# Mirrored blocks of a symmetric product laid out by VectorE before their way through HBM, with new buffer limits and due times of the planner

## The chip, the cores and the metric

One of the eight cores of a Trainium2 chip runs the kernel. The metric is the device time of one launch in microseconds; the time before is the median of three runs, 2388.51 us (2387.62 to 2388.9).

## The reference

Sixteen graphs of 1024 nodes with 128 features go through four layers; each layer normalises x over the features, applies relu, computes something with the graph's 1024 x 1024 adjacency matrix and adds the result to x. All is float32. What matters here:

```python
# layer 0, three times (i = 0, 1, 2), relu after all but the last
h   = h @ W + b
nh  = h / max(norm(h), EPS)
cos = einsum('bij,bkj->bik', nh, nh)            # symmetric, 1024 x 1024
h   = einsum('bpq,bqc->bpc', edge_weight * cos, h)
# layer 1: y = relu(((1 + eps) x + adj^T x) @ W1 + b1) @ W2 + b2
# layer 2: softmax of tanh(s1_i + s2_j) where adj > 0, times h
# layer 3
e   = einsum('bil,bkl->bik', h @ A, h)
e   = e + swapaxes(e, 1, 2)                      # symmetric, 1024 x 1024
att = softmax(where(adj > 0, e, 0), axis=1) * adj
h_prime = relu(einsum('bij,bjk->bik', att, h))   # then three gates of x and h_prime
```

So four times in each graph a symmetric 1024 x 1024 product is formed: in layer 0 for i = 0, 1, 2 and in layer 3.

## The kernel before, in words

Work is tiled in 128 x 128 blocks: a graph has 8 row blocks (index j), and every row of blocks is handled in two halves of four blocks (s = 0 and 1, 512 columns, one PSUM bank). The stages of a graph are named in the plan: T (the transposed adjacency, `adjT`), 0 with 00, 01, 02 (layer 0 and its three products), 1, 2 and 3 (the other layers).

In a product stage 00, 01 or 02 the chain is this. `project` (L1200) multiplies the transposed activations `hT` with the weights, in two halves `psP` of four blocks; VectorE scales them into `h` (L1244; L1547 in stage 00); TensorE transposes each half (`flip`, L1169, into `ps_hTn`) and ScalarE copies it out as `hTn` (L1222). `Square.row` (L1360) multiplies block j of `hTn` with the columns from the diagonal on. VectorE weights each half with the norms and `adjT` into `ew` (L1589), and `accumulate` (L1422) adds it into `acc`, one bank for each half of the columns; in stage 02 `accumulate_nodes` (L1433) does it in blocks. When the eighth `ew` is in, ScalarE copies each half of `acc` out as the `hT` of the next stage (L1222), and `project` begins again. Layer 3 does the same with `e3` (L1854, by the masks) in place of `ew`.

The blocks below the diagonal are not multiplied again. They come in two ways. Those in the four diagonal quarters are copied to `above` by ScalarE (L1392) and transposed by TensorE (L1370). The 16 blocks of the lower left quarter go, for all products of graphs 1 to 13, through VectorE and HBM: for j = 0 to 3 and s = 1, `Square.keep` transposes the 32 x 32 squares of four blocks with one VectorE instruction (L1382); after each odd j, `Square.send` writes two rows of blocks to HBM (L1402, one DMA of 512 KB, called `by_hbm`), and reads them back so that each square lies in its place (L1413, four DMAs of 128 KB, 32 partitions each, into `got`). For j = 4 to 7 and s = 0, `ew` or `e3` reads `got` in place of a PSUM bank. The pieces written are 512 bytes long, the pieces read back 128 bytes, 32 elements.

The transposed adjacency of a later graph comes the same way: four DMAs of 128-byte pieces for each row block (L1509), then a VectorE transpose of the squares in place (L1517) and a ScalarE pass that sums the rows (L1520).

The order of all work is made when the program is built, by the class `Plan`. Every piece of work is an `Op` with an engine, a cost in microseconds, what it reads and writes, and a due time: `graph * PERIOD + TIMES[name][n]`. `Plan.order` goes forward in model time; of the engine whose next work can start first it takes, among the ops that can start within `WINDOW`, the one that is due first. A buffer comes from a pool (`POOLS`), and `KINDS` says how many of a kind may be in use in all and by graphs later than the oldest unfinished one. The result is one list; each engine gets its instructions in that order, and waits for what they read. `TIMES` has entries of their own for the first two and the last two graphs.

Of the kernel before, what the change touches and what calls it, by code (L numbers as in the profile page):

```python
# [12 lines left out]
ALU = mybir.AluOpType  # L13
AX = mybir.AxisListType

P = 128
# [205 lines left out]
def tile_adj_preln(  # L222
# [102 lines left out]
    for load_it in first:  # L325
# [13 lines left out]
        "adjT": ("adjT", 16, 16), "adjL": ("adjL", 5, 5), "x": ("x", 3, 3), "w4": ("big", 11, 5),  # L339
        "chunk": ("big", 13, 11), "above": ("above", 2, 2), "got": ("got", 1, 1), "ps": ("bank", 8, 7),  # L340
        "acc": ("bank", 8, 7), "small": ("small", 7, 18), "row": ("row", 5, 6), "hbm": ("hbm", 3, 3),
# [5 lines left out]
        "T DMA raw <0": [49.7, -29.05, 16.55, 2.15, 37.95, 6.2, 10.3, 13.25],  # L347
        "T PE raw <0": [7.8, -3.3, -0.1, -1.05, 0.65, 10.35, 23.15, 14.4, 9.05, 23.7, 22, 29.65, 26.65, 30.6,
            38.9, 41],
        "T ACT adjT <0": [2.9, 32.7, 7.85, 8.05, 13.45, 9.6, 13.2, 15.2, 18.4, 28.65, 29.8, 34.35, 33.9,  # L350
            38.45, 39.6, 39.65],
        "T DVE su <0": [54],
        "x DMA x <0": [49.15, -28],
        "0 DVE st <0": [5.7, 4.2],
        "0 DVE mv <0": [9.65],
        "0 POOL rstd <0": [2.6],
        "0 DVE nb <0": [9.1],
        "0 DVE hn <0": [9.1],
        "0 ACT hn <0": [30.5],
        "0 PE ps <0": [-0.85, -4.05],  # L360
        "0 ACT hT <0": [-21.45, 7.65],
        "00 PE psP <0": [6.6, -12.45],
        "00 DVE h <0": [14.75, 13.15],
        "00 PE ps <0": [21.35, 2.95],
        "00 ACT hTn <0": [11.15, 11.6],
        "00 ACT sq <0": [5.15, 12.1],
        "00 DVE ss <0": [2.95, 17.5, 18.2],
        "00 POOL rn <0": [30.3],
        "00 PE sq <0": [4.2, 22.45, 6.05, 6.9, 12, 7.4, 9.35, -26.35, 5.2, 26.95, 20.6, 21.8, 29.65, 25.9,
            26.55, 27.25, 31.3, 42.4, 46.3, 24.05, 51.65, 46.5],  # L370
        "00 ACT above <0": [12.45, 21.55, 15.8, 17.1, 16.7, 22.75, 22.65, 30.8, 38.15, 35.2],
        "00 DVE ew <0": [20.65, 22.5, 22.6, 36.95, 26.95, 33.7, 29.1, 35.05, 29.6, 44.15, 35.25, 41.45, 48.8,
            51.7, 45.3, 54.4],
        "00 PE acc0 <0": [0, 11.1, 10.4, 9.05, 15.65, 16.65, 19.7, 23.2, 28.65, 45.65, 34.25, 39.85, 31.35,
            54.3, 44.2, 64.05],
        "00 POOL params <0": [35.05, 40.7, 43.85, 51.55, 56.35, 57.25, 76.7],
        "00 DMA params <0": [52.85],
        "00 DVE params <0": [65.65, 68.1, 68.15, 77.5, 77.95],
        "00 PE params <0": [50.55, 59.35, 66.9],
        "00 ACT hT <0": [51.3, 54],  # L380
        "01 PE psP <0": [47.6, 63.65],
        "01 DVE h <0": [69.95, 78.75],
        "01 PE ps <0": [61.05, 52.95],
        "01 ACT hTn <0": [69.25, 72.45],
        "01 ACT sq <0": [69.7, 71.15],
        "01 DVE ss <0": [76.45, 78.15, 75.45],
        "01 POOL rn <0": [84.25],
        "01 PE sq <0": [68.25, 64.9, 66.25, 69.95, 68.2, 60.6, 70.8, 71.45, 81.95, 78.25, 78.75, 81.15,
            80.55, 85.85, 84.35, 87.05, 85.5, 86.8, 87.75, 84.5, 87.75, 79.1],
        "01 ACT above <0": [72.2, 74.55, 76.2, 75.5, 83.2, 81.35, 84.35, 84.75, 92.9, 94.75],  # L390
        "01 DVE ew <0": [78.15, 92.4, 81.55, 86.8, 87.85, 85.5, 93, 91.7, 93.05, 101.05, 89.5, 98.7, 96.5,
            111.15, 94.25, 91.55],
        "01 PE acc0 <0": [72.7, 84, 78.85, 78.6, 79.65, 78.25, 84.45, 78.05, 85.7, 85.9, 84.65, 87.6, 87.45,
            91.5, 89.15, 92.05],
        "01 ACT hT <0": [97, 99.95],
        "02 PE psP <0": [92.4, 92.15],
        "02 DVE h <0": [111.65, 105.7],
        "02 PE ps <0": [94.65, 94.55],
        "02 ACT hTn <0": [109.1, 104.6],
        "02 ACT sq <0": [106.2, 98.2],  # L400
        "02 DVE ss <0": [108.35, 109.3, 110.85],
        "02 POOL rn <0": [131.5],
        "02 PE sq <0": [103.1, 100.15, 107.65, 110, 101.65, 105.05, 100.95, 91.9, 107.7, 108.8, 108.7, 114,
            114.45, 111, 117.45, 118.85, 121.8, 110.4, 111.4, 123.9, 120.8, 128.25],
        "02 ACT above <0": [109.85, 113, 103.2, 116.3, 113.65, 115.55, 120.5, 124.45, 131.85, 139.8],
        "02 DVE ew <0": [113.25, 106.15, 118, 112.45, 125.7, 120.05, 121.65, 124.9, 130.25, 128.35, 126.65,
            132.8, 124.95, 126.9, 123, 141.6],
        "02 PE acc0 <0": [90.15, 114.45, 106.85, 103.9, 110.45, 112.95, 116.3, 111.45, 125.35, 117.1, 121.95,
            130.1, 112.45, 124.05, 123.15, 120.6],
        "02 DVE x <0": [136.55, 141.55],  # L410
        "T DMA adjT <1": [-129, -138.55, -158.15, -107.7, -154.45, -138.3, -107.8, -104.7],
        "T DVE adjT <1": [-118.3, -111.9, -110.5, -104.85, -101.8, -89, -85.8, -85.05],
        "T ACT adjT <1": [-117.75, -118.25, -112.75, -111.85, -103.3, -98.6, -96, -94.9],
        "1 DVE st <0": [135.95, 138.05],
        "1 DVE mv <0": [141.5],
        "1 POOL rstd <0": [134.7],
        "1 DVE nb <0": [144.5],
        "1 DVE hn <0": [140.8],
        "1 ACT hn <0": [134.3, 134.75],
        "1 DVE x <0": [146.55, 166.45, 168],  # L420
        "1 DMA adjL <0": [49.7, 59.55, 62.4, 63.35, 48, 159, 152, 151.35],
        "1 DVE adjL <0": [80.85, 77.2, 82.45, 79, 78.25, 151.75, 156.5, 161.35],
        "1 PE acc1 <0": [134.5, 135.3, 136.2, 137, 138.5, 133.15, 142.35, 139.75, 142.8, 141.1, 147.5,
            146.05, 148.15, 145.4, 151.95, 150.35],
        "1 ACT g <0": [157.9, 152.5],
        "1 PE py <0": [148.1, 149.8, 154.65, 147.75],
        "1 ACT y1 <0": [150.4, 163, 157.05, 152.1],
        "1 PE py2 <0": [152.35, 154.2],
        "2 DVE st <0": [171.4, 171.55],
        "2 DVE mv <0": [176.05],  # L430
        "2 POOL rstd <0": [176.55],
        "2 DVE nb <0": [173.9],
        "2 DVE hn <0": [173.85],
        "2 ACT hn <0": [184, 172.8],
        "2 PE ps <0": [162, 177.1],
        "2 ACT hnT <0": [180.45, 171.9],
        "2 DVE alone <0": [56.3],
        "2 DVE x <0": [183.6, 216.45, 216.65],
        "2 PE psP <0": [180.2, 166.35, 167.75],
        "2 ACT h <0": [176.5, 180.2, 180.6],  # L440
        "2 DVE hrow <0": [176.1],
        "2 PE pf <0": [171.3],
        "2 ACT hfl <0": [183.15],
        "2 PE pt <0": [174.35],
        "2 ACT sr <0": [180.15],
        "2 DMA sd <0": [283.8],
        "2 DMA s1 <0": [230.2],
        "2 DVE h <0": [175.5],
        "2 ACT e2 <0": [186.9, 189.9, 184.6, 189.95, 190.8, 191.25, 189.25, 193.65, 194, 192.5, 194.7, 197.1,
            198.05, 200.15, 199.1, 197.05],  # L450
        "2 DVE e2 <0": [195.1, 187.55, 193.65, 194.5, 199.55, 199.6, 196.4, 198.2, 201.75, 200.6, 203.8,
            206.9, 206.25, 208.1, 207.45, 208.75],
        "2 PE acc2 <0": [186.85, 186.2, 184.15, 189.1, 194.4, 197.45, 194.9, 188.8, 187.75, 198.65, 189.3,
            188.2, 194.8, 201.05, 196.95, 200.75, 197.1, 199.85, 195.55, 197.6, 198.5, 195, 197.75, 199],
        "2 DVE rden <0": [210.05, 211, 214.85, 213.35],
        "3 DVE st <0": [214.65, 213.1],
        "3 DVE mv <0": [246.2],
        "3 POOL rstd <0": [230.15],
        "3 DVE nb <0": [191.15],
        "3 DVE hn <0": [197.2],  # L460
        "3 ACT hn <0": [220.35, 225.45],
        "3 PE ps <0": [220.35, 209.3, 217.3, 213.95],
        "3 ACT hnT <0": [217.95, 221.55],
        "3 PE pg <0": [214.85, 222.65],
        "3 ACT gT <0": [221.05, 225.75],
        "3 PE psP <0": [228.55, 206.05, 224.15],
        "3 DVE h <0": [228.15, 223.85, 227.05],
        "3 ACT h3T <0": [219.7, 220],
        "3 ACT mask <0": [8.25, 18.4, 14.05, 26, 16.05, 23.05, 27.85, 30.25, 28.2, 40.5, 248.85, 250, 222.55,
            229.15, 237.05, 239.9],  # L470
# [679 lines left out]
    def by_block(t, w=D, n=NB):  # L1150
        return t[:, 0 : n * w].rearrange("p (c d) -> p c d", d=w)
# [976 lines left out]
```

## Time and profile before, and how to read it

| | before |
|---|---|
| median of 3 runs | 2388.51 us |
| the profiled execution | 2389.48 us, span 2387.7 us |
| TensorE matmul busy | 2349.2 us, 98% of the span |
| VectorE busy | 2029.0 us, 85% |
| ScalarE busy | 1435.5 us, 60% |
| the 52 mirrored products through HBM: writes / reads | 104 DMAs of 512 KB / 416 of 128 KB |
| packets under 512 B / all | 1108441 / 1316743 |
| a steady graph, 617.3 to 1917.1 us, nine of them | 144.4 us |

The span runs from the first to the last instruction. A busy engine's records can overlap, so that what TensorE loses is better read from the starts: a record of a 512-column matmul normally starts 0.429 us after the one before (each float32 matmul has two records), one of 128 columns 0.111, a transpose of a block 0.109. What a start comes later than that is called a stall below. The first TensorE record starts 7.3 us after the span's start, the last ends 10.5 us before its end, and the stalls of over 0.02 us in between sum to 44.6 us.

### The profile page before, as it was taken

The page shows a single profiled execution, that of the slowest core. Times are in us where ns is not written, and L with a number is a line of the kernel's source. Part 1 is how long each engine was busy: PE and PEld are TensorE (multiplying, and loading weights), DVE is VectorE, ACT ScalarE, POOL GpSimd, SP SyncE. Part 2 cuts the span into 40 slices and gives each one's busy share as a digit, 9 for nine tenths or more (in the row PEclk, how much of TensorE's full clock was granted, in tenths as well). Part 3 has the DMA queues.
Part 4 walks back from the last instruction along what each step waited for, and adds up shares of the span by engine and source line. Part 5 has one row for each costly group of instructions (what it writes and reads, how often), then busy time and mean ns, then how long its engine had stood idle before and what let it go on. Part 6 is the DMA issues. An engine that isn't in the chain of part 4 may idle for free.

```text
span 2387.7 us, 35098 instructions
## 1 busy us (share of the span) xinstructions
PE 2349.2 (98%) x11577; PEld 1548.5 (65%) x11577; DVE 2029.0 (85%) x5570; ACT 1435.5 (60%) x2561; POOL 246.8 (10%) x168
## 2 busy tenths in 40 slices
PE   8999999999999999999999999999999999999997
PEld 5568566675766657666575666757576575765764
DVE  6658798898988989899898988989899888987676
ACT  7325765756566465755756657465765656655475
POOL 3001010100101101010100101001011010110012
PEclk9999999999999999999999999999999999999999
DMA  9342949879596886959779497796968869165000
GB/s 197 85 107 63 172 91 180 153 128 178 115 177 141 139 171 130 171 123 166 157 129 181 108 181 146 137 164 130 171 139 149 164 129 169 45 107 124 1 27 18
DMA packets 1316743, 314.31 MB, mean 132 GB/s; under 512 B 1108441, under 2 KB 1298017, under 8 KB 1316561
## 3 DMA queue, kind: packets, MB, share of 16 engines
q1 hardware_dynamic: 1296400, 301.35, 67.6%
q10 hardware_dynamic: 19264, 9.70, 1.4%
q8 instruction: 92, 1.51, 0.3%
q0 software_dynamic: 896, 1.01, 0.2%
q14 instruction: 91, 0.74, 0.1%
HBM read 227.50 MB, written 84.47 MB: 131 GB/s over the span
## 4 chain that ended last, share of the span: by engine, by line
PE 85%; DMA 5%; SPq 4%; ACT 3%; DVE 3%; issue 1%; DVEq 0%; ACTq 0%
PE acc L1422 33%; PE sq L1360 18%; PE acc L1433 17%; PE psP L1200 6%; PE sq L1370 4%; DMA by_hbm<-above 2%; PE py L1210 2%; DMA got<-by_hbm 2%; PE py L1651 2%; SPq L1413 1%; SPq L1509 1%; PE ps_hTn L1169 1%; PE pg L1210 1%; DVE ew L1589 1%; DMA adjT<-in_adj_dram 1%
## 5 line engine op out<-in xcount | busy, mean ns | idle before, releaser
L1422 PE MATMUL acc<-ew,h 128*128 128x512 f32 x1024 | 486.4, 597 | 8.0 <-DVE ew L1589 8.0
L1589 DVE SCALAR_TENSOR_TENSOR ew<-sq,rn,adjT 128x512 f32<-128x512 f32 x612 | 436.4, 740 | 59.4 <-PE sq L1370 24.4
L1360 PE MATMUL sq<-hTn 128*128 128x512 f32 (+3 forms) x1152 | 439.4, 488 | 0.8 <-ACT hTn L1222 0.4
L1392 ACT COPY above<-sq 128x384 f32<-128x384 f32 (+3 forms) x432 | 167.6, 393 | 365.1 <-PE sq L1370 263.1
L1360 PEld LDWEIGHTS sq<-hTn 128*128 128x128 f32 x1152 | 196.3, 191 | 148.0 <-issue 99.8
L1422 PEld LDWEIGHTS acc<-ew,h 128*128 128x128 f32 x1024 | 180.2, 191 | 169.9 <-issue 132.4
L1433 PEld LDWEIGHTS acc<-h,ew 128*128 128x128 f32 x2048 | 245.4, 192 | 35.9 <-issue 21.7
L1433 PE MATMUL acc<-h,ew 128*128 128x128 f32 x2048 | 253.3, 275 | 3.2 <-DVE ew L1589 3.2
L1433 PEld LDWEIGHTS acc<-h,e 128*128 128x128 f32 x2048 | 235.0, 192 | 17.2 <-issue 12.8
L1422 PE MATMUL acc<-e,hs 128*128 128x512 f32 x512 | 241.1, 594 | 1.3 <-ACT hs L1904 0.8
L1433 PE MATMUL acc<-h,e 128*128 128x129 f32 x2048 | 236.6, 275 | 1.1 <-DVE e L1763 1.1
L1422 PE MATMUL acc<-adjL,hn 128*128 128x512 f32 x512 | 232.9, 592 | 0.0
L1162 POOL TENSOR_TENSOR rstd<-ve,mhalf 128x8 f32<-128x8 f32 x64 | 105.0, 1641 | 1166.5 <-DVE ve L1281 1166.5
L1370 PEld LDWEIGHTS sq<-ident,above 128*128 128x128 f32 x960 | 124.4, 141 | 100.2 <-issue 76.5
L1854 DVE CUSTOM_DVE_ANT_0 e<-mask,sq 128x512 f32<-128x512 int8 x204 | 137.4, 680 | 60.6 <-ACT above L1392 53.2
L1520 ACT ACTIVATE adjT<-adjT 128x1024 f32<-128x1024 f32 x120 | 126.6, 1055 | 97.8 <-DVE adjT L1517 90.4
L1895 DVE TENSOR_TENSOR e<-e,adjT 128x512 f32<-128x512 f32 x248 | 166.1, 680 | 18.2 <-ACT e L1886 18.1
L1382 DVE STREAM_TRANSPOSE above<-sq 128x512 f32<-128x512 f32 x208 | 145.7, 706 | 35.5 <-PE sq L1360 35.5
L1370 PE MATMUL sq<-ident,above 128*128 128x128 f32 x960 | 172.5, 273 | 1.5 <-ACT above L1392 1.5
L1763 DVE SCALAR_TENSOR_TENSOR e<-adjT,e 128x512 f32<-128x512 f32 x256 | 162.3, 689 | 5.5 <-ACT e L1759 5.3
L1422 PEld LDWEIGHTS acc<-adjL,hn 128*128 128x128 f32 x512 | 93.6, 190 | 102.3 <-issue 90.9
L1517 DVE STREAM_TRANSPOSE adjT<-adjT 128x1024 f32<-128x1024 f32 x120 | 148.6, 1239 | 8.8 <-DMA adjT<-in_adj_dram 8.4
(164 smaller groups left out, 3587.2 us busy)
## 6 DMA issues: line engine op xcount, KB each, us to landing
adjL<-in_adj_dram SPq DMA_DIRECT2D x128, 512.0 KB
adjT<-in_adj_dram SPq DMA_DIRECT2D x480, 128.0 KB
by_hbm<-above SPq DMA_DIRECT2D x104, 512.0 KB
got<-by_hbm SPq DMA_DIRECT2D x416, 128.0 KB
s<-sd SPq DMA_DIRECT2D x15, 512.0 KB
out_dram<-z ACTq DMA_DIRECT2D x15, 512.0 KB
d_hT<-hn SPq DMA_DIRECT2D x14, 512.0 KB
hT<-d_hT SPq DMA_DIRECT2D x56, 128.0 KB
```

The costliest lines, as they stand in the source:

```text
L1200: nc.tensor.matmul(dst.t[:, (c - lo) * n : (c - lo + 1) * n], cols(srcT.t, c), w, start=True, stop=True)
L1360: lambda: nc.tensor.matmul(dst.t[:, (first - lo) * P :], cols(leftT.t, j), span(rightT.t, first, hi), start=True, stop=True),
L1370: nc.tensor.transpose(cols(dst.t, r), cols(above.t, p), ident)
L1382: lambda: nc.vector.transpose(span(above.t, p, p + 4), read.t),
L1392: lambda: nc.scalar.copy(span(above.t, p, p + hi - first), read.t[:, (first - lo) * P :]),
L1422: lambda s=s, lo=lo, hi=hi: nc.tensor.matmul(acc[s].t, cols(h.t, at, w), span(ew.t, lo, hi), start=(j == 0), stop=(j == NB - 1)),
L1433: nc.tensor.matmul(a.t[:, (c - lo) * n : (c - lo + 1) * n], cols(ew.t, c), h.t[:, at * w : at * w + n], start=(j == 0 and c == lo), stop=( ...
L1517: dve(V(N), [t], [t], lambda t=t: nc.vector.transpose(t.t, t.t), True)
L1589: lambda view=view, ew=ew, rn=rn, j=j, lo=lo, hi=hi: nc.vector.scalar_tensor_tensor(by_block(span(ew.t, lo, hi), D, 4), view(), rn.t[:, j ...
L1763: lambda e=e, j=j, lo=lo, hi=hi: nc.vector.scalar_tensor_tensor(span(e.t, lo, hi), span(aT[j].t, lo, hi), 0.0, span(e.t, lo, hi), op0=ALU. ...
L1854: lambda e=e, view=view, mask=mask, peak=peak, s=s, lo=lo, hi=hi: nc.vector.tensor_tensor_reduce(by_block(span(e.t, lo, hi), D, 4), by_blo ...
L1895: lambda e=e, j=j, lo=lo, hi=hi: nc.vector.tensor_mul(span(e.t, lo, hi), span(e.t, lo, hi), span(aT[j].t, lo, hi)),
```

## The change

Three parts.

1. VectorE's transpose of the squares (L1382, new L1385) reads and writes in another order: the four squares of a 32-row group that belong to one destination row group lie side by side in `above`, so that one piece of HBM holds runs for all four blocks. The write to HBM is as before in size and pieces (128 x 8 x 128). The read back has four DMAs as before, with pieces of 128 elements, 512 bytes, in place of 32 elements: the listing of the built program shows `got<-by_hbm 32x8x128 x4` for `32x32x32 x4`.
2. `got` then holds runs of 32 columns, which `ew` and `e3` read as 16 runs of 32 elements; a helper `like` gives the output and the other operand the same shape. No instruction is added for it. The planner's cost of the read falls from 3.6 to 1.8 for two rows.
3. All due times in `TIMES` and several limits in `KINDS` are new, so that the planner makes another order of the same work. In the listing TensorE has the same instructions as before, in another order; VectorE, ScalarE and GpSimd too, and the DMAs of the SP queue. In the steady graphs the order repeats from graph to graph, in both kernels.

```diff
-        "adjT": ("adjT", 16, 16), "adjL": ("adjL", 5, 5), "x": ("x", 3, 3), "w4": ("big", 11, 5),
-        "chunk": ("big", 13, 11), "above": ("above", 2, 2), "got": ("got", 1, 1), "ps": ("bank", 8, 7),
-        "acc": ("bank", 8, 7), "small": ("small", 7, 18), "row": ("row", 5, 6), "hbm": ("hbm", 3, 3),
+        "adjT": ("adjT", 16, 16), "adjL": ("adjL", 5, 5), "x": ("x", 3, 3), "w4": ("big", 9, 5),
+        "chunk": ("big", 10, 12), "above": ("above", 2, 1), "got": ("got", 1, 1), "ps": ("bank", 7, 8),
+        "acc": ("bank", 7, 8), "small": ("small", 7, 16), "row": ("row", 3, 3), "hbm": ("hbm", 3, 3),
...
-        "T DMA raw <0": [49.7, -29.05, 16.55, 2.15, 37.95, 6.2, 10.3, 13.25],
+        "T DMA raw <0": [51.6, -92.65, -42.9, 3.5, 39.85, 7.55, 4, 14.6],
...
+    def like(v, t):
+
+        return t.rearrange("p (x i) -> p x i", i=v.shape[2])
...
-                return self.got, lambda: self.got.t.rearrange("p (r c d) -> p c r d", r=QUARTER, d=P)[:, q]
+                return self.got, lambda: self.got.t.rearrange("p (x q i) -> p q x i", q=QUARTER, i=SQ)[:, q]
...
-                    lambda: nc.vector.transpose(span(above.t, p, p + 4), read.t),
+                    lambda: nc.vector.transpose(
+                        self.apart(j // 2).rearrange("p (h r q i) -> p r h q i", r=2, q=QUARTER, i=SQ)[:, j % 2],
+                        read.t.rearrange("p (q h i) -> p h q i", h=P // SQ, i=SQ),
+                    ),
...
+        def apart(self, pair):
+
+            return span(self.above.t, 6 + 8 * pair, 14 + 8 * pair)
...
-                src = by_hbm.t.rearrange("(x j) (g i) -> g j x i", j=SQ, i=SQ)
-                for g in range(P // SQ):
-                    dst = span(got.t, lo * 4, hi * 4)[g * SQ : (g + 1) * SQ]
-                    with nc.allow_non_contiguous_dma(reason="squares"):
-                        nc.sync.dma_start(dst.rearrange("p (x i) -> p x i", i=SQ), src[g])
-
-            op("DMA", 1.8 * (hi - lo), [by_hbm], [blk(got, lo * 4, hi * 4)], squares_to_places, lat=2.4)
+                src = by_hbm.t.rearrange("(h y j) f -> h j y f", h=P // SQ, j=SQ)
+                dst = by_block(span(got.t, lo * 4, hi * 4))
+                for h in range(P // SQ):
+                    nc.sync.dma_start(dst[h * SQ : (h + 1) * SQ], src[h])
+
+            op("DMA", 1.8, [by_hbm], [blk(got, lo * 4, hi * 4)], squares_to_places, lat=2.4)
...
-                            by_block(span(ew.t, lo, hi), D, 4), view(), rn.t[:, j : j + 1],
-                            by_block(span(aT[j].t, lo, hi), D, 4), op0=ALU.mult, op1=ALU.mult,
+                            like(view(), span(ew.t, lo, hi)), view(), rn.t[:, j : j + 1],
+                            like(view(), span(aT[j].t, lo, hi)), op0=ALU.mult, op1=ALU.mult,
```

TensorE's order in the steady graph 7, from the listing of the two built programs, where stage 01 begins (`acc0_7_0_1` is the second half of stage 00's sum, `psP_7_1_1` the second half of stage 01's projection, `ps_hTn_7_1_1` its transposes; names with 6 belong to layer 2 of the graph before):

```
before                                        after
acc0_7_0_1 <- ew_7_0_7   (the last one)        acc0_7_0_1 <- ew_7_0_6
ps_hnT_6_2_1 x4                                pt_6
psP_6_2_0 x3                                   ps_hTn_7_1_0 x4
psP_7_1_1 x4                                   acc0_7_0_1 <- ew_7_0_7   (the last one)
ps_hTn_7_1_0 x4                                psP_7_1_1 x4
psP_6_2_3 x3                                   ps_hTn_7_1_1 x4
psP_6_2_6 x2                                   sq_7_1_0_0
ps_hTn_7_1_1 x4                                sq_7_1_0_1
```

## The prediction

> **What bounds the kernel now.** I read the page first: the share of each engine and the chain that ended last.
>
> ```profile
> span 2387.7 us, 35098 instructions
> PE 2349.2 (98%) x11577; PEld 1548.5 (65%) x11577; DVE 2029.0 (85%) x5570; ACT 1435.5 (60%) x2561; POOL 246.8 (10%) x168
> PE 85%; DMA 5%; SPq 4%; ACT 3%; DVE 3%; issue 1%; DVEq 0%; ACTq 0%
> ```
>
> TensorE is busy for 98% and carries 85% of the chain. A busy record can hide a stall, so I went to the starts of the records: a 512-column record normally starts 0.429 us after the last, a 128-column one 0.111, a transpose 0.109. Summing what comes later than that gives 44.6 us of stalls, with 7.3 us before the first record and 10.5 after the last; the other 2325 us are streaming, which the change leaves alone, since TensorE's instructions are the same. So a gain can at most be some of 44.6 us, while a worse order has no such limit. Next, the busy time by stretches, one row for each steady graph:
>
> ```profile
> core 0: us, PE busy (x) PEld busy (x) DVE busy (x) ACT busy (x) POOL busy (x), PEclk, DMA share, GB/s
> 906.61:1050.37 143.76, 143.51 (x705) 94.42 (x705) 128.80 (x353) 89.66 (x158) 13.36 (x8) 1.00 0.81 150
> 1050.37:1195.95 145.58, 144.07 (x705) 94.32 (x705) 128.85 (x353) 88.95 (x158) 13.36 (x8) 1.00 0.85 149
> ```
>
> A graph takes 144.4 us on average; VectorE works 128.8 of it, so it has 15 us of room, and the 16 DMA engines are 81 to 85% busy. The stalls of these nine graphs are 0.7 to 2.5 us each. What makes them is in the timeline. A trip to ScalarE and back that is partly covered, 0.44 us of TensorE work lying between (graph 5, stage 02; the same in every steady graph):
>
> ```profile
> 783.73 2.74 PE L1422 MATMUL acc<-ew,h 128*128 128x512 f32 x6
> 786.31 0.60 PE L1169 MATMUL ps_hTn<-ident,h 128*128 128x128 f32 x4
> 787.16 2.94 PE L1200 MATMUL psP<-w,hT 128*128 128x128 f32 x24 [0.25 <-ACT hT L1222]
> ```
>
> The four transposes take 0.44 us; the projection starts 0.85 us after them, 0.41 more than normal. The same trip with nothing between, at the end of graph 14:
>
> ```profile
> 2334.76 4.45 PE L1422 MATMUL acc<-e,hs 128*128 128x512 f32 x10
> 2339.25 1.08 ACT L1222 ACTIVATE hpT<-acc 128x512 f32<-128x512 f32 x2 [7.61 <-PE acc L1422]
> 2339.89 2.05 PE L1200 MATMUL psN<-eye,hpT 128*128 128x131 f32 x16 [0.69 <-ACT hpT L1222]
> ```
>
> Here the stall is 0.85 us. And a trip to VectorE with four blocks' instructions, in graph 2, stage 01:
>
> ```profile
> 309.85 2.04 PE L1200 MATMUL psP<-w,hT 128*128 128x128 f32 x16
> 311.03 2.16 DVE L1244 SCALAR_TENSOR_TENSOR h<-psP,rn,b 128x128 f32<-128x128 f32 x8 [0.30 <-PE psP L1200]
> 311.73 1.85 PE L1169 MATMUL ps_hTn<-ident,h 128*128 128x128 f32 x8
> ```
>
> Eight transposes are normally 0.87 us of starts and end at 1.03; they take 1.85, because each waits for its block of `h`. Last, the mirrored blocks, late in graph 1:
>
> ```profile
> 58.20 7.13 SPq L1413 DMA_DIRECT2D got<-by_hbm  x8
> 69.48 2.74 DVE L1589 SCALAR_TENSOR_TENSOR ew<-got,rn,adjT 128x512 f32<-128x512 f32 x4 [8.23 <-DMA got<-by_hbm]
> 70.28 2.07 PE L1422 MATMUL acc<-ew,h 128*128 128x512 f32 x2 [4.25 <-DVE ew L1589]
> ```
>
> Eight reads keep the SP queue for 7.13 us, VectorE waits 8.23 us for them, and TensorE stalls 4.47 us. After that five records of 512 columns start 0.85 us apart.
>
> **What the Trainium skill says.** "DMA: Bandwidth & Descriptors", Specifications: 512 bytes is the smallest transfer at line rate. The packet records agree in kind: a 128-byte packet took 15.6 ns on average, a 512-byte one 28.5, so four times the bytes for 1.8 times the time. "Perfetto Trace Analysis", DMA Instruction (HWDGE): the issue's recorded span ends when the descriptors are made, not at the landing; here VectorE starts 4 us after the last of the eight issues. "TensorE: Matmul & The Clock Gate", Part 1 (The HAM clock gate): after an idle window of some 3.4 us the clock is halved until TensorE has been busy again; the five records at twice their time after 4.47 us agree. "SBUF — State Buffer", Door 1 (The DMA port swizzle): full bandwidth needs further accesses within a 16-byte line; runs of 32 elements (128 bytes) fill whole lines. No row of this trace reads or writes in runs of 32.
>
> **The change part by part.**
>
> *Transfers.* The 416 reads drop from 1024 packets to 256 each. For one pair of rows: 4096 x 15.6 / 16 = 4.0 us of the DMA engines becomes 1024 x 28.5 / 16 = 1.8; the four issues, 3.12 us at the median, become perhaps 4 x 0.39 = 1.6 (0.39 is the median issue of the 512-byte writes). The two overlap, so the way gets 1.6 to 2.2 us shorter. In a steady graph the first user in stage 00 has 12.3 us of TensorE work as lead and stalls for 0 to 0.8, so the way is 12.3 to 13.1 long; it becomes about 10.9. The new order gives it 11.2. That covers it, and I let all stalls at `got` in steady graphs go: 6.8 us in nine graphs, 0.76 each. At the head, eight issues fall from 7.1 to about 3.1 us; the lead falls from 13.0 to 11.8; the stall goes from 4.5 to 1.7, and with it the slow clock (5 x 0.42 = 2.1): a gain of 4.9. In graph 2, stage 01, the lead falls from 18.1 to 8.2 us; against 10.9 this costs some 2.5.
>
> *VectorE.* 16 transposes and 16 reads of `got` in a graph keep their counts. I take their rows (0.706, 0.748, 0.680 us); a gain is excluded, as engine, type and number of elements are the same, and above I keep twice the row.
>
> *Order.* Hidden or not is a matter of lead: the TensorE work that its own order puts between what a trip starts from and what waits for it. From the listing, a steady graph after the change has, with the prices above (first record and following ones):
> - stage 01, second half of `psP` directly behind the last `acc`: lead 0, 0.85 + 0.11 = 0.96;
> - stage 01, second half's transposes directly behind that: at lead 0.44 the case of graph 2 cost 0.15 + 0.45 = 0.60, so at lead 0 1.04;
> - stage 02, `psP` behind `acc` again: 0.96;
> - stage 02, transposes with lead 0.44: 0.60;
> - stage 00, a transposed block with lead 0.64: 0.14, as at the same lead in graph 1.
>
> Sum 3.70 us. Before there is one such place, 0.53. Work lies ready in neither case: in the new order nothing else stands between on TensorE's queue, and all behind waits. On VectorE's queue the second `h` of stage 01 now stands behind sums, statistics and aggregates of the next graph (0.68 + 0.10 + 4 x 2 x 0.21 + 0.64 + 0.17 = 3.3 us since the last `ew`, against 1.06 + 0.85 + 0.89 = 2.8 for TensorE's side), so it is 0.4 to 0.5 late; in stage 02 0.2. I add 0.5, bounds 0 and 0.7. Net for a steady graph: 3.70 + 0.5 - 0.53 - 0.76 = 2.9. Graphs 5 to 13: 9 x 2.9 = 26.2.
>
> *The other graphs*, by the same list: graph 2 3.7 + 2.5 against 4.1 (+2.1), graph 3 2.2 against 1.3 (+0.9), graph 4 2.8 against 0.7 (+2.1); graphs 0 and 1 +1.5 and the head's -4.9; graph 14 -0.3; graph 15 +1.7 (short leads around `ps_hTn`). Together +3.1. The last 10.5 us, and SP's moved loads (its issues shrink by 8 x 1.6 us a graph), I cost at nothing: the tail's instructions keep their order, and the loads have leads of tens of us.
>
> Sum: 26.2 + 3.1 = 29.3, on the profiled execution's 2389.5: 2418.8. That execution is 1.0 above the median, so 2417.8; I take 2418. Bounds: VectorE's lateness -4.5 to +2, head and graph 2 +-5, graph 15 +-4, so 2404 to 2436.
>
> **The rivals.**
> - *Faster: shorter transfers outweigh the bare trips.* Place: the users of `got`, and the small gaps of some 0.9 us a graph that VectorE, waiting 22.7 us for `got` in all, may be causing. Price: 11.8 us of stalls, 2.1 of slow clock, and up to 14 of small gaps, 28 together. It decides if the bare trips cost less than that, that is under some 2 us a graph; at half my price (18 in all) the time is 2378. For it speaks that the DMA engines are over 80% busy; against it that the trips are measured with the same instructions in the same trace, and that the small gaps stand at record boundaries.
> - *The reads do not get shorter* (landing, not packets, sets them). Then the lead of 11.2 is 1.1 short, and the 0.76 stays: 9 x 1.9 = 17, graph 2 another 2, the head 6: 2443. Against it: eight issues alone took 7 us.
> - *Runs of 32 make VectorE slow.* It decides from (147.3 - 128.8) / 32 = 0.58 us for each of the 32 instructions; at twice their rows VectorE has 151 us a graph, 13 x 7 us more: 2480. Against it: runs of 128 from `got` took 0.748 where runs from PSUM took 0.740.
> - *Nothing to be seen*: losses and gains cancel, 2388.
>
> **How the numbers follow.** Bare trips 0.81 (2418, own range 2404 to 2436), reads not shorter 0.08, faster 0.05, VectorE bound 0.04, cancelled 0.02. Leaving out all but the first keeps 0.81, so its range is the range. Within 0.2% (4.8 us, about what a measurement of this kernel can tell) I put 0.03.
>
> **What would show it.** Steady graphs of about 147.3 us; in each, `psP` twice with an idle time of some 0.7 us ended by ScalarE's `hT`, and `ps_hTn` ended by VectorE's `h` right behind; waits for `got` near zero; the four read issues at 1.6 us or less; `ew<-got` and the transposes at their old means. Steady graphs at 144.4 or below would prove the trips wrong, `got` waits of 1 us a graph the transfers, VectorE means above 0.9 us its pattern.

## The result, and the profile after

The changed kernel takes 2543.82 us (median of six runs, 2541.32 to 2547.84), the kernel before, beside it, 2388.7; the ratio is 1.065 [1.0635, 1.0662], so it is 155 us slower where 29 were forecast. The profiled execution took 2543.01 us. The new lines are 3 to 9 below the old ones. The page again first, its span, engines and chain:

```profile
span 2541.1 us, 35091 instructions
PE 2405.7 (95%) x11577; PEld 1565.6 (62%) x11577; DVE 2041.0 (80%) x5570; ACT 1438.4 (57%) x2561; POOL 251.0 (10%) x168
PE 71%; DVE 10%; DMA 7%; ACT 6%; SPq 3%; issue 2%; DVEq 0%; POOL 0%; ACTq 0%
```

No engine has much more to do, and TensorE's share of the chain fell from 85 to 71%: the time is in waits. By the starts of TensorE's records it is all there: the first starts at 7.25 us, the last ends at 2530.5, and the stalls of over 0.02 us sum to 198.2 (44.6 before), which leaves 2325.0 us of streaming, for 2325.3 before. By the graph whose work waits:

| TensorE's stalls, us | before | after | difference | forecast |
|---|---|---|---|---|
| graphs 0 to 4 | 21.7 | 96.1 | +74.4 | +1.7 |
| graphs 5 to 13 | 12.8 | 79.5 | +66.7 | +26.2 |
| graphs 14 and 15 | 10.0 | 22.6 | +12.6 | +1.4 |

Busy time by stretches, a steady graph and then the longest one of the start, from the first matmul of one graph's stage 00 to that of the next; the row after that is the same stretch of the start in the kernel of experiment 1, which has the new layout in the old order (by the counts of TensorE's records, 955 and 1005, the two stretches of the start do not hold quite the same work):

```profile
1617.34:1769.09 151.75, 147.10 (x705) 95.44 (x703) 128.57 (x349) 89.47 (x157) 13.41 (x8) 0.99 0.70 143
154.80:361.58 206.78, 190.78 (x955) 129.38 (x954) 150.25 (x425) 119.08 (x204) 15.98 (x9) 0.96 0.47 109
```

```profile
150.39:351.09 200.70, 198.92 (x1005) 132.58 (x1004) 163.13 (x469) 123.10 (x213) 16.94 (x10) 1.00 0.50 116
```

The steady graph was forecast at 147.3; graphs 5 to 13 take 152.1 on average. VectorE works 128.6 us in the one shown, as before, and the DMA engines are busy for 70%. Where it waits, the timeline of TensorE and then that of ScalarE show for graph 11, between stages 01 and 02:

```profile
1779.70 1.45 PE L1431 MATMUL acc<-ew,h 128*128 128x512 f32 x3
1783.55 1.16 PE L1203 MATMUL psP<-w,hT 128*128 128x128 f32 x8 [2.40 <-ACT hT L1225]
1784.54 1.71 PE L1172 MATMUL ps_hTn<-ident,h 128*128 128x128 f32 x8
```

```profile
1780.18 0.63 ACT L1575 ACTIVATE sq<-h 128x512 f32<-128x512 f32 x1 [2.47 <-DVE h L1247]
1780.85 1.65 ACT L1308 ACTIVATE hn<-x,nb,rstd 128x128 f32<-128x128 f32 x4
1782.40 0.61 ACT L1329 ACTIVATE hn<-hn 128x512 f32<-128x512 f32 x1
1782.92 0.57 ACT L1225 ACTIVATE hT<-acc 128x512 f32<-128x512 f32 x1
```

The copy `hT` that TensorE waits for is ready to go soon after the last `acc`, but five instructions `hn` of the graph before stand ahead of it. The wait at `got` has not gone either. The issues of its reads, its users on VectorE (shortest, median and longest one in ns), and what VectorE sat idle for before them (us, times), before and then after:

```profile
L1413 SPq DMA_DIRECT2D got<-by_hbm x416: 302/650/3469, 58.2 to 2135.1; - x139
  DMA got<-by_hbm: 22.7, 18
```

```profile
L1422 SPq DMA_DIRECT2D got<-by_hbm x416: 302/448/1927, 59.4 to 2274.8; - x139
L1598 DVE SCALAR_TENSOR_TENSOR ew<-got,rn,adjT x156: 710/747/767, 70.2 to 2115.8; 128x512 f32<-128x512 f32 x156
  DMA got<-by_hbm: 37.3, 19
```

The median issue of a read falls to 0.448 us (0.650 before), and the four of a pair to 1.80 (3.11); the aggregates, `ew` from `got`, take 0.747 us as before (0.748); but VectorE waits 37.3 us for `got`, where it was 22.7.

### The profile page after: what moved, and what is told of

It reads as the page before. It is cut to its first block, busy times and chain, and to the rows that moved or that the text cites. A ratio compares the mean times of both kernels' runs of the same rounds, so it can differ in the third digit from the quotient of the medians.

```text
span 2541.1 us, 35091 instructions
## 1 busy us (share of the span) xinstructions
PE 2405.7 (95%) x11577; PEld 1565.6 (62%) x11577; DVE 2041.0 (80%) x5570; ACT 1438.4 (57%) x2561; POOL 251.0 (10%) x168
## 4 chain that ended last, share of the span: by engine, by line
PE 71%; DVE 10%; DMA 7%; ACT 6%; SPq 3%; issue 2%; DVEq 0%; POOL 0%; ACTq 0%
PE acc L1431 27%; PE sq L1363 16%; PE acc L1442 14%; PE psP L1203 5%; PE sq L1373 3%; DVE ew L1598 3%; DMA by_hbm<-above 2%; SPq L1518 2%; DMA got<-by_hbm 2%; ACT e L1764 2%; PE py L1213 1%; PE ps_hTn L1172 1%; DVE x L1247 1%; ACT hn L1308 1%; DVE h L1247 1%
## 5 line engine op out<-in xcount | busy, mean ns | idle before, releaser
L1431 PE MATMUL acc<-ew,h 128*128 128x512 f32 x1024 | 499.9, 606 | 33.9 <-DVE ew L1598 33.4
L1363 PE MATMUL sq<-hTn 128*128 128x512 f32 (+3 forms) x1152 | 447.0, 493 | 0.2 <-ACT hTn L1225 0.2
L1442 PEld LDWEIGHTS acc<-h,e 128*128 128x128 f32 x2048 | 243.4, 195 | 42.0 <-DVE e L1772 20.1
L1442 PE MATMUL acc<-h,e 128*128 128x129 f32 x2048 | 248.0, 279 | 18.4 <-DVE e L1772 18.3
L1385 DVE STREAM_TRANSPOSE above<-sq 128x512 f32<-128x512 f32 x208 | 146.5, 707 | 54.3 <-PE sq L1363 54.0
```

Of the source, the lines that this page charges most:

```text
L1363: lambda: nc.tensor.matmul(dst.t[:, (first - lo) * P :], cols(leftT.t, j), span(rightT.t, first, hi), start=True, stop=True),
L1385: lambda: nc.vector.transpose(self.apart(j // 2).rearrange("p (h r q i) -> p r h q i", r=2, q=QUARTER, i=SQ)[:, j % 2], read.t.rearrange(" ...
L1431: lambda s=s, lo=lo, hi=hi: nc.tensor.matmul(acc[s].t, cols(h.t, at, w), span(ew.t, lo, hi), start=(j == 0), stop=(j == NB - 1)),
L1442: nc.tensor.matmul(a.t[:, (c - lo) * n : (c - lo + 1) * n], cols(ew.t, c), h.t[:, at * w : at * w + n], start=(j == 0 and c == lo), stop=( ...
```

## The experiments

Theory 1: the order loses the time, and the layout gains a little. Theory 2: the layout loses it. Then, within theory 1: why is the order poor, the due times (1b) or the price that the planner takes for a read (1a)? The limits play no part: with the old `KINDS` the changed kernel gets the same order on every engine.

**1. Layout alone**: the old `TIMES`, `KINDS` and planner's prices under the new transposes, DMAs and views; against the changed kernel:

```diff
-            op("DMA", 1.8, [by_hbm], [blk(got, lo * 4, hi * 4)], squares_to_places, lat=2.4)
+            op("DMA", 1.8 * (hi - lo), [by_hbm], [blk(got, lo * 4, hi * 4)], squares_to_places, lat=2.4)
...
-        "T DMA raw <0": [51.6, -92.65, -42.9, 3.5, 39.85, 7.55, 4, 14.6],
+        "T DMA raw <0": [49.7, -29.05, 16.55, 2.15, 37.95, 6.2, 10.3, 13.25],
...
```

> The new layout (transposes, writes, reads of 512-byte pieces, columns in runs of 32) with the old due times, limits and planner's costs: the listing of this kernel has the order of the kernel before on every engine. Theory 1 (the new order loses the time, the layout gains a little): the waits at got of the steady graphs and of the head go, 2374 to 2387 us. Theory 2 (the layout itself loses it: the reads land later, or runs of 32 hold VectorE up): 2450 to 2545. If the reads are shorter but their landing is as late as before: 2386 to 2391.

2377.67 us (2376.41 to 2377.88), ratio 0.995 [0.9939, 0.9964]. Theory 2 is out: the layout alone is 11 us, 0.5%, faster. Waits for `got` on VectorE are down to 8.2 us in all, 7.0 of them in the head; a steady graph takes 143.70 us (1214.26 to 1357.96), 0.7 less than before.

**2. Order alone**: the changed kernel's order with the old transposes, DMAs and views; against the kernel before:

```diff
-            op("DMA", 1.8 * (hi - lo), [by_hbm], [blk(got, lo * 4, hi * 4)], squares_to_places, lat=2.4)
+            op("DMA", 1.8, [by_hbm], [blk(got, lo * 4, hi * 4)], squares_to_places, lat=2.4)
...
-        "T DMA raw <0": [49.7, -29.05, 16.55, 2.15, 37.95, 6.2, 10.3, 13.25],
+        "T DMA raw <0": [51.6, -92.65, -42.9, 3.5, 39.85, 7.55, 4, 14.6],
...
```

> The old layout (128-byte pieces read, planner's prices as in the changed kernel) in the order of the changed kernel on every engine. Theory 1 (order): at least the changed kernel's time, and 1 to 2 us more in each of graphs 1 to 13, since the way through HBM is some 2 us longer and its lead of 11.2 us was already short: 2545 to 2580. Theory 2 (layout): near the kernel before, 2390 to 2440.

2622.94 us (2614.01 to 2636.8), ratio 1.098 [1.0951, 1.1017]: theory 1, and with more than I had expected. In an order with short leads the slower reads cost 79 us, VectorE waiting 90.2 us for `got`; in the old order they cost 11.

**3. The changed kernel with the price of 3.6.**

```diff
-            op("DMA", 1.8, [by_hbm], [blk(got, lo * 4, hi * 4)], squares_to_places, lat=2.4)
+            op("DMA", 3.6, [by_hbm], [blk(got, lo * 4, hi * 4)], squares_to_places, lat=2.4)
```

> The changed kernel with one number back: the planner's price of the read of two rows is 3.6 again, not 1.8; layout, due times and limits stay the new ones. In its listing a steady graph has no bare trip but the one that the kernel before has, and the first user of got has a lead of 12.9 us. Theory 1a (the due times belong to the price of 3.6; at 1.8 the planner puts other work into the freed time of the SP queue and all that follows moves): steady graphs of 143.5 to 144.2 us, 2365 to 2385 in all. Theory 1b (the due times themselves are poor, whatever the price): 2480 to 2545. Theory 2 (layout): 2500 to 2545.

2382.99 us (2380.86 to 2385.34), ratio 0.9975 [0.9965, 0.9985]. One number of the planner, which no instruction carries, is worth 161 us. A steady graph:

```profile
1213.86:1357.55 143.69, 143.44 (x705) 94.55 (x704) 129.39 (x352) 89.34 (x158) 13.36 (x8) 1.00 0.72 151
```

So the new due times are good ones at the price of 3.6 (1a); 1b is out.

**4. The kernel before with the price of 1.8**: old layout, old due times.

```diff
-            op("DMA", 1.8 * (hi - lo), [by_hbm], [blk(got, lo * 4, hi * 4)], squares_to_places, lat=2.4)
+            op("DMA", 1.8, [by_hbm], [blk(got, lo * 4, hi * 4)], squares_to_places, lat=2.4)
```

> The kernel before with one number changed: the planner's price of the read of two rows is 1.8, not 3.6; old layout, old due times and limits. Theory 1a (a fitted set of due times goes with the prices it was fitted to): slower than before although no instruction is added, 2410 to 2480. Theory 1b: within 10 us of before, 2380 to 2400, since its due times are good ones; its listing has one more partly bare trip in a steady graph, 0.14 us.

2504.6 us (2498.52 to 2511.0), ratio 1.049 [1.0461, 1.0513]; more than I had put. The old due times do not bear the price of 1.8 either. But in the old layout this price is also too low, as the four issues of a read take 3.1 us, and VectorE waits 48.4 us for `got` where it was 22.7; so a part of these 116 us can come from there. The old due times at 1.8 with the new layout were not run. The combinations that were:

| due times | price 3.6 | price 1.8 |
|---|---|---|
| old | 2388.6 old layout, 2377.7 new layout | 2504.6 old layout |
| new | 2383.0 new layout | 2543.8 new layout, 2622.9 old layout |

The price itself is not false: the four issues of a read take 1.80 us in the trace. What matters is that the due times go with it. `Plan.order` first asks what can start, and only among that within 0.05 us does the due time choose. With a read half as long, the DMA queue of the model is free earlier, while the second write has not landed, and other work is put in; this is a reading of the planner's rule, and the lists fit it. The SP queue in the head is the first place where the orders at the two prices part. In experiment 3 eight reads follow each other:

```profile
57.84 5.33 SPq L1422 DMA_DIRECT2D got<-by_hbm  x8
63.26 1.82 SPq L1476 DMA_DIRECT2D adjL<-in_adj_dram  x4
```

In the changed kernel a load goes between, and in the listings TensorE's and VectorE's orders part within the same few microseconds:

```profile
59.41 2.13 SPq L1422 DMA_DIRECT2D got<-by_hbm  x4
61.64 0.40 SPq L1476 DMA_DIRECT2D adjL<-in_adj_dram  x1
63.33 1.78 SPq L1422 DMA_DIRECT2D got<-by_hbm  x4
```

**5. One wait on ScalarE's queue taken away.** The finished list is edited, and nothing else:

```diff
+    for b in range(4, 13):
+        late, early = find[b, "01 ACT hT", 1], find[b - 1, "3 ACT hn", 0]
+        ordered.remove(late)
+        ordered.insert(ordered.index(early), late)
```

> The changed kernel with one ScalarE instruction moved in its list, in graphs 4 to 12: the copy of the second half of stage 01's hT goes ahead of the five hn instructions of the graph before, all else as it was. Theory 1 (my price of the bare trip left out what stands ahead on ScalarE's queue): the wait of the second psP of stage 02 falls from 2.7 to 3.5 us to the 0.97 of graphs 2, 3 and 13, where hn does not stand ahead: 9 trips, 17 us in all, 2522 to 2531 us. Rival (the copy waits for something else, or hn then holds up layer 3): 2540 to 2547.

2542.9 us (2536.26 to 2545.49), ratio 1.064 [1.0621, 1.0658]. The trip, TensorE's wait at the second `psP` of stage 02, did fall to 0.97 us in all nine graphs, as priced, and the time did not: of the 17 us taken away there, 13 came back at the first sums of stage 02, some 1.5 us a graph where nothing had waited, and more at the users of `got`. VectorE's timeline shows what stands ahead:

```profile
1782.87 1.25 DVE L1194 STREAM_TRANSPOSE hTn<-hTn 128x1024 f32<-128x1024 f32 x1 [0.74 <-DMA hTn<-d_hTn]
1784.04 0.65 DVE L1581 TENSOR_REDUCE ss<-sq 128x4 f32<-128x512 f32 x1
```

The sum of squares, on which the norms and so all of stage 02's `ew` depend, stands behind a transpose for the next graph that waits for a transfer.

**6. Loads behind the read**, with VectorE's two users of them behind the users of `got`, in graphs 5 to 13:

```diff
+        for key, nths, behind in (("1 DMA adjL", (4, 3, 2), ("00 DMA got", 1)), ("1 DVE adjL", (2, 3), ("00 DVE ew", 13))):
+            for n in nths:
+                o = find[b, key, n]
+                ordered.remove(o)
+                ordered.insert(ordered.index(find[(b, *behind)]) + 1, o)
```

> The changed kernel with the three 512 KB loads of adjL that stand around the second write of stage 00 put behind the read of got, in graphs 5 to 13, and the two VectorE instructions that use them put behind the users of got. Theory 1 (the write waits behind two loads in the DMA queue: its read is issued 6.0 us after it, 3.5 in the kernel with the old order and the new layout): the read is issued 3.5 to 4 us after the write, the wait of the first user in stage 00 falls from 1.3 to 2.8 us to 0 to 0.6, 2528 to 2537 us. Rival (the landing does not depend on what was queued before): 2541 to 2547.

2534.88 us (2533.31 to 2539.94), ratio 1.061 [1.0598, 1.0629]: as theory 1 has it. The SP queue of graph 8 in the changed kernel, then here:

```profile
1251.23 1.35 SPq L1476 DMA_DIRECT2D adjL<-in_adj_dram  x2
1252.84 0.38 SPq L1412 DMA_DIRECT2D by_hbm<-above  x1
1253.31 0.53 SPq L1476 DMA_DIRECT2D adjL<-in_adj_dram  x1
1258.84 1.81 SPq L1422 DMA_DIRECT2D got<-by_hbm  x4
```

```profile
1250.20 0.39 SPq L1412 DMA_DIRECT2D by_hbm<-above  x1
1253.47 1.80 SPq L1422 DMA_DIRECT2D got<-by_hbm  x4
1255.37 1.34 SPq L1476 DMA_DIRECT2D adjL<-in_adj_dram  x3
```

The read can be issued when the write has landed: 6.0 us after the write's issue where two loads of 512 KB had been issued in the 1.6 us before it and one behind it, 3.3 without the three. Over graphs 5 to 13 it was 4.0 to 6.5 us, 5.3 in the mean, and is 3.2 to 3.8 here. Which of the three counts most was not tried apart; in experiment 1 the seven pairs with one such load behind the write and none in the 2 us ahead of it take 3.5 to 4.7 us. The Trainium skill, "DMA: Bandwidth & Descriptors", Queues, rings and completion order, says that each DMA engine takes descriptors in ring order; these lines agree. The wait of the first user falls from 1.3 to 2.8 us to 0.9. What is left could be VectorE's order: it takes row 7 of `ew` (0.7 us) ahead of row 4, which TensorE needs first.

**7. Both edits, and row 4 ahead of row 7:**

```diff
+        late, early = find[b, "00 DVE ew", 14], find[b, "00 DVE ew", 8]
+        ordered.remove(late)
+        ordered.insert(ordered.index(early) + 1, late)
```

> The two edits before together, and the aggregate of row 7 put behind that of row 4 on VectorE, which TensorE waits for first. If the terms add: steady graphs of 147.5 to 148.5 us, near the 147.3 that the prediction had, 2505 to 2517 us. If the waits only move to the next place: above 2525.

2528.39 us (2527.07 to 2530.93), ratio 1.0586 [1.0569, 1.0604]: 15 us off, where 27 to 39 would have been the sum: the wait at stage 02's first sums, some 1.4 us a graph, stays as in experiment 5, and the third edit gains nothing at `got`: 0.90 and 0.27 us of waits at two sums become 0.24, 0.46 and 0.47 at three.

**8. The price of 3.6 from graph 5 on.**

```diff
-            op("DMA", 1.8, [by_hbm], [blk(got, lo * 4, hi * 4)], squares_to_places, lat=2.4)
+            op("DMA", 3.6 if now[0] > 4 else 1.8, [by_hbm], [blk(got, lo * 4, hi * 4)], squares_to_places, lat=2.4)
```

> The changed kernel with the planner's price of the read at 3.6 for the products of graphs 5 to 15 and 1.8 for graphs 1 to 4. Theory 1 (every place where the price and the due times disagree costs by itself): graphs 5 to 13 of 143.7 to 144.3 us, the start as poor as in the changed kernel: 2455 to 2475 us. Rival (the start throws the later graphs off their due times): graphs of 150 us and more, 2520 to 2545.

2459.54 us (2456.38 to 2460.09), ratio 1.029 [1.0276, 1.0307]: graphs 6 to 13 take 143.7 to 143.9 us each although the start is as poor as in the changed kernel. The loss is made graph by graph.

**9. Experiment 7 with the transpose behind the sums of squares.**

```diff
+        late, early = find[b + 1, "00 DVE hTn", 0], find[b, "02 DVE ss", 2]
+        ordered.remove(late)
+        ordered.insert(ordered.index(early) + 1, late)
```

> The changed kernel with the three edits of the run before, and VectorE's transposes of the next graph's hTn (stage 00), which wait for a transfer, put behind the sums of squares ss of stage 02, which TensorE's first sum of stage 02 waits for by way of the norms, in graphs 4 to 12. Theory 1 (the wait that left the second psP went to the next in-order queue, VectorE's): the waits of 1.07 and 0.44 us at the first sums of stage 02 fall to 0.3 or less together, 2514 to 2521 us. Rival (they wait for something else, or move on again): 2525 to 2531.

2515.53 us (2513.18 to 2518.34), ratio 1.053 [1.0517, 1.0546]. The waits at stage 02's first sums are gone, and this time nothing took their place: the wait of experiment 5 had moved from ScalarE's queue to VectorE's. The nine graphs from 5 on now take 149.2 us on average (701.9 to 2044.96).

**10. Graph 4's reads first on the SP queue:**

```diff
+    for late, early in ((("00 DMA got", 0), ("00 DMA by", 1)), (("00 DMA got", 1), ("T DMA adjT", 5))):
+        late, early = find[(4, *late)], find[(4, *early)]
+        ordered.remove(late)
+        ordered.insert(ordered.index(early) + 1, late)
```

> The changed kernel with one move on the SP queue, in graph 4 alone: the reads of got of stage 00 go ahead of the loads of adjT 5 to 7 and of one adjL, where they stand behind 13 issues. Theory 1 (at the start as in the steady graphs, it is the loads put ahead on the DMA queue that make the lead too short): the wait of 6.2 us at graph 4's first user of got falls below 2, and the slow clock after it goes; 2535 to 2540 us. Rival (that TensorE's order leaves it no work, whenever the reads land): 2541 to 2547.

2544.18 us (2540.89 to 2545.63), ratio 1.065 [1.0635, 1.0664]: no gain; the stall stays at 6.0 us. The reads were issued by 640.2, and VectorE came to the aggregate at 652.71 without a wait, its list being full.

**11. The price of 3.6 up to graph 4**, the counterpart of experiment 8 (`1.8 if now[0] > 4 else 3.6`).

> The changed kernel with the planner's price of the read at 3.6 for graphs 1 to 4 and 1.8 from graph 5 on. If start and steady graphs are separate losses, this takes away what the kernel with 3.6 from graph 5 on kept, 76 us: 2460 to 2475 us, steady graphs still of 151 to 152 us. If the start threw the rest off: 2383 to 2420.

2470.84 us (2465.23 to 2479.72), ratio 1.035 [1.0324, 1.0373]. The start is worth 73 us and the rest 84 (experiment 8), together 157 of the 161 of experiment 3.

**12. The best version with one trip covered**: experiment 1, with the next graph's first `psP` put ahead of stage 02's second, in graphs 2 to 13:

```diff
+        late, early = find[b, "02 PE psP", 1], find[b + 1, "00 PE psP", 0]
+        ordered.remove(early)
+        ordered.insert(ordered.index(late), early)
```

> The new layout in the old order, with one swap in TensorE's list in graphs 2 to 13: the first half of the next graph's psP goes ahead of the second half of stage 02's, so that the one partly bare trip of a steady graph, 0.53 us, has 1.33 us of work as lead. If it is covered and the second transposes keep enough of theirs (0.89 us of lead for 1.79): 2370 to 2374 us, graphs of 143.2. If the wait moves to those transposes: 2376 to 2380.

2379.64 us (2378.93 to 2381.63), ratio 0.996 [0.9951, 0.9976]. The 0.53 us at `psP` are gone; 0.3 stand at the moved `psP` instead, and 0.3 more at the transposes and products behind. No gain, so experiment 1 is the version to keep, faster than both kernels.

**13. Graph 4's reads and its first aggregate first**, experiment 10 with this as well:

```diff
+    late, early = find[4, "00 DVE ew", 8], find[3, "2 DVE mv", 0]
+    ordered.remove(late)
+    ordered.insert(ordered.index(early), late)
```

> As the run with graph 4's reads put first, and on VectorE graph 4's aggregate of row 4 (the first user of got, for which TensorE waits) put ahead of the statistics, gates and transposes that stand before it: in that run the reads had been issued by 640.2 us, and VectorE came to the aggregate at 652.7 without a wait. Theory (two things held the same place, the reads on the SP queue and then VectorE's own queue): the wait of 6.0 us falls below 1, the slow clock after it goes too, 2533 to 2538 us. Rival (the read lands late all the same, or another place waits instead): 2541 to 2546.

2544.91 us (2542.66 to 2549.44), ratio 1.066 [1.0638, 1.0673]: the rival holds. The wait at the first user of `got` falls from 6.0 to 0.1 us, and TensorE stops a little later for as long:

```profile
647.95 1.12 PE L1431 MATMUL acc<-ew,h 128*128 128x512 f32 x2
648.91 0.81 PE L1363 MATMUL sq<-hTn 128*128 128x384 f32 x2
655.76 0.48 PE L1373 MATMUL sq<-ident,above 128*128 128x128 f32 x1 [6.04 <-ACT above L1398]
```

ScalarE's copy `above` stands behind a pass over `adjT` that itself waits for VectorE. Here no single wait carries the loss: TensorE's list reaches this stretch before the other engines' lists do. That the other places of the start are like this one is not shown.

## Why the prediction was wrong, step by step

*Direction right, size wrong*: 155 us for 29.

*Range*: its upper end was also added up wrongly: the terms given for it, +2, +5 and +4, lead to 2429, not 2436. The time lies far above either.

*TensorE bounds, its streaming stays*: right, 2325.3 us and 2325.0.

*Transfers*: right in the steady graphs, where the order leaves them their lead: with the layout alone TensorE's stalls in graphs 5 to 13 fall from 12.8 to 5.5 us, by 7.3 for the 6.8 forecast, with four issues at 1.8 us where I had 1.6 at most. Wrong at the head, where I forecast eight issues of 3.1 us and a gain of 4.9. In experiment 1 the eight take 5.59 us and TensorE still waits 2.98 us for the first aggregate (4.25 before); in the changed kernel, the last line here, it waits 4.62, so that nothing is gained:

```profile
58.53 5.59 SPq L1423 DMA_DIRECT2D got<-by_hbm  x8
68.03 2.74 DVE L1599 SCALAR_TENSOR_TENSOR ew<-got,rn,adjT 128x512 f32<-128x512 f32 x4 [7.03 <-DMA got<-by_hbm]
68.83 2.08 PE L1432 MATMUL acc<-ew,h 128*128 128x512 f32 x2 [2.98 <-DVE ew L1599]
```

```profile
71.05 2.08 PE L1431 MATMUL acc<-ew,h 128*128 128x512 f32 x2 [4.62 <-DVE ew L1598]
```

That my 11.7 us in all lie near the 10.9 that experiment 1 gained is luck. And "The new order gives it 11.2. That covers it" failed: in the mean of graphs 5 to 13 the first user of `got` waits 1.64 us and the next 0.33, where they had waited 0.32 and 0.06, which I let go to nothing. The step that failed here is "SP's moved loads", which I cost "at nothing": they went around the write and made the way from its issue to the read's 2.0 us longer in the mean, 5.3 for 3.3 (experiment 6). I had looked at their own leads, not at what is queued behind them.

*VectorE*: right as a bound and for its rows. Transposes 0.707 us, aggregates 0.747, with masks 0.677.

*Order, the bare trips*: four of five prices right, in means of graphs 5 to 13: second `psP` of stage 01 0.97 (forecast 0.96), transposes behind it 1.06 (1.04), those of stage 02 0.54 (0.60), the transposed block 0.09 (0.14). The fifth, stage 02's `psP`, was mis-sized: 2.68 for 0.96. My price came from the end of graph 14, where ScalarE had nothing else to do; here `hn` stands ahead. The trace has its own control: in graphs 2, 3 and 13 of the changed kernel, where `hn` is elsewhere, the same trip takes 0.97. The Trainium skill, "Perfetto Trace Analysis", Tensor Engine Instruction, says that ScalarE, VectorE and GpSimd are strict first-in, first-out queues; experiments 5 and 9 agree, and I had applied that to VectorE alone. With both terms mended for the most part (experiment 9), 149.2 us are left for my 147.3; the four trips make up 3.6 of the 6.2 us of stalls in it, and the rest are waits of under 0.5 us each in the mean, 1.2 of them at `got`, that I had no row for.

*VectorE 0.5 late*: not seen where I put it; the transposes of stage 01 wait 1.06 us, and I had 1.04 for them without this term.

*The other graphs, +3.1*: this failed by most; 87 us were measured. "By the same list" I priced only trips of one step and the ways to `got`, and of those the one in graph 2, stage 01, stalls TensorE for 4.95 us where I had 2.5. The largest stall, in graph 1, is of another kind:

```profile
319.30 1.10 PE L1172 MATMUL ps_hTn<-ident,h 128*128 128x128 f32 x4 [0.45 <-DVE h L1247]
330.62 1.66 PE L1442 MATMUL acc<-h,e 128*128 128x129 f32 x6 [10.22 <-DVE e L1772]
```

Layer 2's scores pass through HBM, the weights `e` made of them through ScalarE and VectorE, and the new list leaves TensorE nothing to do meanwhile. Stalls of over 3.4 us alone sum to 42.6 us in graphs 1 to 4 (one of 4.5 before), and slow records follow them: those of 129 columns behind this wait start 0.21 us apart for a normal 0.11, and the clock column of that stretch has 0.96. Two more stalls, 3.3 and 3.4 us, stand in graphs 14 and 15, where TensorE waits for ScalarE's `hs`.

*Rivals*: that the reads do not get shorter is refuted by their issues and by experiment 1, that runs of 32 are slow by VectorE's rows, and that shorter transfers win by the time itself; they do gain, but 11 us only. The case that came true was none of mine: the price change, which I had described in one sentence and costed nowhere, goes with due times fitted to another price. That they were fitted at 3.6 is inferred from experiment 3, not read anywhere.

*Open*: how the 74 us of the start divide among places. Two attempts at one of them (10, 13) moved the wait and not the time; only the price, which changes the whole list, takes it away.

## What to carry to other kernels

A cost that a planner uses is part of its fitted schedule: change it, even to the truer value, and the due times may have to be fitted again (not tried here), or keep the old one and change the emission alone, which here is the fastest kernel. When pricing a round trip by its lead, read the list of every engine and DMA queue on the way, and count what stands ahead of each step. A wait removed by hand in a poor order tends to reappear one queue further: expect a gain only when the next step on that path is early, too.

## What the runs showed of the hardware

From the issue of a write of 512 KB to HBM to the issue of the read that depends on it, on the same queue, the shortest of 104 pairs took 3.20 to 3.21 us in all of the kernels before, after and experiments 1 to 3, whatever the layout. In graphs 5 to 13 of the changed kernel, with loads of 512 KB issued around the write, the pair of stage 00 took 4.0 to 6.5 us, and 3.2 to 3.8 with these loads moved behind the read. I had priced the read's pieces, and not this part of the way.
